# The gate with one column tile per pair and one transposition, the last group's results stored by halves, and another order of GpSimd's work, in a two-layer conditioned block

## The chip, the core and the metric

The kernel runs on one core of a Trainium2 chip, as one launch. The metric is the device time of one execution in microseconds (us). Everything is fp32. A profile of one execution is at hand for the kernel before. In it the engines are called PE (TensorE, the matmuls), PEld (PE's weight loads), DVE (VectorE), ACT (ScalarE), POOL (GpSimd) and SP (the engine that issues most DMAs).

## What is computed

The input x is 128 samples of 64 channels by 1024 positions. Two layers follow each other, each with a residual:

```
x = x + ffn0(cond0(x))      # cond0: per-sample 64x64 channel mix; ffn0: rank-128 linear, plus a bias
x = x + ffn1(cond1(x))      # cond1: grouped conv of 9 taps, plus a context per sample
def ffn1(y):                # per row of 1024
    logits = y @ gate_w.T + expert_bias          # 4 experts
    one_hot = first maximum of logits
    z = y @ lora_A.T                             # 4 experts x rank 8
    return y @ W_up.T + (z * one_hot) @ lora_B
```

The change concerns ffn1: the gate (logits and z, then the choice of the expert), and how the results of ffn1 are added to x and stored.

## The kernel before

**Tiles.** Two samples make a "pair" tile of 128 rows by 1024; there are 64 pairs. Two pairs make a group d, and the main loop (L778) runs over 32 groups. PE's order, like that of every engine, is the order in which the program is written (`manual_schedule`): nothing is moved by a scheduler, and a wait at the head of an engine's queue holds back all behind it.

**One pass of the loop.** For group d it runs: the second matmul of layer 0 for pair 2d+5 (`layer0_out`, L413); the gate of group d (`gate`, L590); on GpSimd the bias of layer 0 for pairs 2d+6 and 2d+7 (`add_fbias`, L640) and the convolution's differences for pairs 2d+4 and 2d+5 (`differences`, L452); products 8 to 25 of ffn1 for group d (`products`, L542), with the turning of the chosen z (`turn`, L618) ahead of product 23; then `tiles` (L648), which holds the convolution of pairs 2d+4 and 2d+5, the matmuls of the next group's gate (`gate_in`, L571), the low-rank part of group d (`lora`, L625) and the results (`results`, L631); then the sums of the next group (`ffn_sums`, L530), loads two groups on, layer 0 of pairs 2d+6 and 2d+7, and products 0 to 7 of group d+1 in two parts.

**ffn1 by products.** The 1024x1024 weight is not multiplied plainly: a fast scheme of 26 block products of 128x256 (the table `PRODUCTS`, L83) takes sums of blocks of y (made by GpSimd) and sums of blocks of W. Product (r, u, w, ...) goes into part r of eight; two parts share a PSUM bank, so bank 0 holds parts 0 and 1, bank 1 parts 2 and 3, and so on. Banks 0 and 1 are the low and high columns of the first pair, banks 2 and 3 those of the second. Products 0 to 3 of a group open banks 1, 2, 3 and 1 again, in that order. Some products are followed by a copy from one part to another on ACT (`"copy"`), or by an add to x on DVE (`"x"`). Product 19 is followed by an ACT copy of part 0 to part 2. The last products are: 20 to bank 2, 21 to bank 3, 22 and 23 to bank 0, 24 to bank 3 and 25 to bank 1.

**The gate.** `gate_in` (L571) takes `gl`, the 36 columns of gate and lora_A padded to 64, as stationary operand. It has 64 columns, so it fills half of PE's columns, and the other half can work beside it. Eight matmuls, one for each eighth c of the channels, are 256 wide: both pairs. Those with even c go to PSUM rows 0 to 63, those with odd c to rows 64 to 127. So the result is in two halves, which have still to be added. ACT copies 128x256 to SBUF (`gate_out`, L586). `gate` (L590) then runs, for each of the two pairs, a matmul with this copy as stationary operand and `fold` as moving operand, a 128x36 matrix with two ones in each column: it turns rows into columns and adds the halves. Eight small DVE instructions (L598 to L614) choose the expert and mask z.

```
rows = slice(c % 2 * GT, (c % 2 + 1) * GT)                            # L576
nc.tensor.matmul(pt[:, t * GL : (t + 1) * GL], zg[:, t], fold, ...)   # L595
```

**Results.** `lora` adds four matmuls, one for each bank; `results` adds the banks to x on DVE in the order 1, 3, 2, 0, and SP stores each pair whole, 512 KB. The banks of a group have only one buffer, so the next group's product 0 waits for the add of bank 1, product 1 for that of bank 2 and product 2 for that of bank 3.

**GpSimd's queue** holds, for a pass: two biases (each waits for the load of its x), two differences of two instructions (each waits for the convolution's input X, which has gone through DRAM), 17 sums, and the issue of four loads.

Of the kernel before, what the change touches and what calls it, by code (L numbers as in the profile page):

```python
# [35 lines left out]
F32 = mybir.dt.float32  # L36
AF = mybir.ActivationFunctionType
ALU = mybir.AluOpType
# [3 lines left out]
P = 128  # L42
# [4 lines left out]
NC = L // P  # L47
# [7 lines left out]
GL = E + ER  # L55
# [4 lines left out]
GT = 64  # L60
# [49 lines left out]
)  # L110
NW = 26

PK = tuple(np.cumsum([0, P, P, 1, 1, P, 8, 8, CH, CH, E]).tolist())

# [2 lines left out]
def block(ctx: ExitStack, tc: tile.TileContext, a: dict, out: bass.AP):  # L117
    nc = tc.nc
    const = ctx.enter_context(tc.tile_pool(name="const", bufs=1))
# [11 lines left out]
    sp = ctx.enter_context(tc.tile_pool(name="sp", bufs=2))  # L131
# [16 lines left out]
    ident = const.tile([P, P], F32, name="ident")  # L148
    make_identity(nc, ident)

    xs, xts, bds, aggbs, ctxs = {}, {}, {}, {}, {}
# [9 lines left out]
    for i in range(NBD):  # L161
        t = const.tile([P, GP, 2, CH], F32, name=f"bd{i}")
# [46 lines left out]
    for i in range(NX):  # L209
        t = cvp.tile([P, BG, P + 1], F32, tag=f"X{i}", name=f"X{i}")  # L210
# [13 lines left out]
        sel,  # L224
        ident[:, : 2 * FIRST].rearrange("p (t b) -> p t b", b=2).unsqueeze(2).to_broadcast([P, FIRST, CH, 2]),
    )
    fold = const.tile([P, GL], F32, name="fold")
    nc.vector.tensor_tensor(fold, ident[:, :GL], ident[:, GT : GT + GL], ALU.add)
    aggd = dram.tile([NB, CH, CH], F32, name="aggd")
    ctxd = dram.tile([NB, CH], F32, name="ctxd")  # L230
    aggbd = dram.tile([NB, CH], F32, name="aggbd")
# [12 lines left out]
    def load_context(g):  # L244
        load_rows(g, ctxs, ctxd, "cx")
# [138 lines left out]
    lo, hi = slice(0, N), slice(N, L)  # L384
    xbs, z0s, yts, opened = {}, {}, {}, {}
    diffs, pms, m2s, pcs, zgs, ys = {}, {}, {}, {}, {}, {}
# [65 lines left out]
    def differences(pr):  # L452

        xt = X[pr % NX]
        diffs[pr] = tmp.tile([P, BG, 2, H], F32, tag=f"tmp{pr % 2}", name=f"df{pr}")
        at_even, at_odd, after = (
            xt[:, :, s : s + P].rearrange("p g (m two) -> p g m two", two=2)[:, :, :, i]
            for s, i in ((0, 0), (0, 1), (1, 1))
        )
        nc.gpsimd.tensor_tensor(diffs[pr][:, :, 0], at_even, at_odd, ALU.subtract)  # L460
        nc.gpsimd.tensor_tensor(diffs[pr][:, :, 1], after, at_odd, ALU.subtract)
# [80 lines left out]
    def products(d, first, end):  # L542
        if not first:
            opened[d] = [psb.tile([P, N], F32, tag=f"pb{i}", name=f"pb{i}_{d}") for i in range(4)]
        for r, u, w, new, _, then in PRODUCTS[first:end]:
            p = part(d, r)
            if new == 2:
                nc.vector.memset(p, 0.0)
            for c in range(QC):
                nc.tensor.matmul(  # L550
                    p, ys[d][u][:, c], W[:, w, c], start=new == 1 and c == 0, stop=c == QC - 1, skip_group_check=True
                )
            for kind, to, op in then:
                if kind == "dcopy":
                    nc.vector.tensor_copy(part(d, to), p)
                elif kind == "copy" and op == "+":
                    nc.scalar.copy(part(d, to), p)
                elif kind == "copy":
                    nc.scalar.activation(part(d, to), p, AF.Copy, scale=-1.0)
                elif kind == "add":  # L560
                    copy = sums.tile([P, NQ], F32, tag="v", name=f"v{d}_{to}")
                    nc.scalar.copy(copy, p)  # L562
                    combine(nc.vector, part(d, to), part(d, to), op, copy)
                else:
                    x = xs[2 * d + to // 4][:, to % 4 * NQ : (to % 4 + 1) * NQ]
                    if op == "+":
                        nc.vector.tensor_tensor(x, p, x, ALU.add)  # L567
                    else:
                        nc.vector.scalar_tensor_tensor(x, p, -1.0, x, ALU.mult, ALU.add)  # L569

    def gate_in(d):  # L571

        yt = yts[d]
        pg = bank(f"pg{d}")
        for c in range(NC):
            rows = slice(c % 2 * GT, (c % 2 + 1) * GT)  # L576
            nc.tensor.matmul(  # L577
                pg[rows, : 2 * P].rearrange("m (t r) -> m t r", t=2),
                gl[:, c, :],
                yt[:, :, c],  # L580
                start=c < 2,
                stop=c >= NC - 2,
            )
        return pg

    def gate_out(d, pg):  # L586
        zgs[d] = sp.tile([P, 2, P], F32, tag="zg", name=f"zg{d}")
        nc.scalar.copy(zgs[d].rearrange("p t r -> p (t r)"), pg[:, : 2 * P])

    def gate(d):  # L590

        zg = zgs.pop(d)
        pt = bank(f"pgt{d}")
        for t in range(2):
            nc.tensor.matmul(pt[:, t * GL : (t + 1) * GL], zg[:, t], fold, start=True, stop=True)  # L595
        pv = pt[:, : 2 * GL].rearrange("p (t c) -> p t c", t=2)
        lg = sp.tile([P, 2, E], F32, tag="lg", name=f"lg{d}")
        nc.vector.tensor_tensor(lg, pv[:, :, :E], ebias.unsqueeze(1).to_broadcast([P, 2, E]), ALU.add)  # L598
        mx = sp.tile([P, 2], F32, tag="mx", name=f"mx{d}")
        nc.vector.tensor_reduce(mx, lg, AX.X, ALU.max)  # L600
        sc = sp.tile([P, 2, E], F32, tag="sc", name=f"sc{d}")
        nc.vector.tensor_tensor(sc, lg, mx.unsqueeze(2).to_broadcast([P, 2, E]), ALU.is_equal)
        nc.vector.tensor_tensor(sc, sc, rank.unsqueeze(1).to_broadcast([P, 2, E]), ALU.mult)
        ms = sp.tile([P, 2], F32, tag="ms", name=f"ms{d}")
        nc.vector.tensor_reduce(ms, sc, AX.X, ALU.max)
        oh = sp.tile([P, 2, E], F32, tag="oh", name=f"oh{d}")
        nc.vector.tensor_tensor(oh, sc, ms.unsqueeze(2).to_broadcast([P, 2, E]), ALU.is_equal)
        zm = sp.tile([P, 2, 2, E, R], F32, tag="zm", name=f"zm{d}")
        for h in range(2):
            nc.vector.tensor_tensor(  # L610
                zm[:, :, h],
                pv[:, :, E:].rearrange("p t (e r) -> p t e r", e=E),
                oh.unsqueeze(3).to_broadcast([P, 2, E, R]),
                ALU.mult,  # L614
            )
        return zm

    def turn(d, zm):  # L618
        p = bank(f"pzt{d}")
        nc.tensor.transpose(p[:, :P], zm.rearrange("p t h e r -> p (t h e r)"), ident)  # L620
        zt = sp.tile([P, P], F32, tag="zt", name=f"zt{d}")
        nc.scalar.copy(zt, p[:, :P])
        return zt

    def lora(d, zt):  # L625

        for j, p in enumerate(opened[d]):
            rows = slice(j * ER, (j + 1) * ER)
            nc.tensor.matmul(p, zt[rows, :], lb[rows, :], start=False, stop=True, skip_group_check=True)  # L629

    def results(d):  # L631
        p = opened.pop(d)
        xa, xb = xs.pop(2 * d), xs.pop(2 * d + 1)
        for x, cols, b in ((xa, hi, p[1]), (xb, hi, p[3]), (xb, lo, p[2]), (xa, lo, p[0])):
            nc.vector.tensor_tensor(x[:, cols], b, x[:, cols], ALU.add)  # L635
        del yts[d], ys[d]
        nc.sync.dma_start(out[2 * d], xa)
        nc.sync.dma_start(out[2 * d + 1], xb)

    def add_fbias(pr, eng):  # L640
        eng.tensor_tensor(xs[pr], xs[pr], fbias, ALU.add)  # L641
# [67 lines left out]
    gl = loaded("gl", [P, NC, GT], eng=nc.scalar)  # L709
# [66 lines left out]
    zm = gate(0)  # L776
    first_products(2)
    for d in range(NPAIR // 2):  # L778
        more = d + 1 < NPAIR // 2
        ahead = [pr for pr in (2 * d + 6, 2 * d + 7) if pr < NPAIR]  # L780
        if d and 2 * d + 5 < NPAIR:
            layer0_out(2 * d + 5)
        if 2 * d + 5 < NPAIR:
            load_context(d + 2)
        if ahead:
            load_cond(d + 3)
        if d:
            zm = gate(d)
        for pr in ahead:
            add_fbias(pr, nc.gpsimd)  # L790
        for pr in (2 * d + 4, 2 * d + 5):
            if pr < NPAIR:
                differences(pr)
        if d:
            products(d, 8, 23)
        else:
            first_products(2)
        zt = turn(d, zm)
        if d:
            products(d, 23, 26)  # L800
        else:
            first_products(2)
        tiles(d, zt, 2 * d + 4, 2 * d + 5)
        if more:
            ffn_sums(d + 1)
        for pr in (2 * d + 8, 2 * d + 9):
            if pr < NPAIR:
                load_x(pr)
        for pr in ahead:
            layer0_in(pr)  # L810
        if ahead:
            layer0_mix(ahead[0])
        if more:
            products(d + 1, 0, 4)
        if ahead:
            layer0_out(ahead[0])
            layer0_mix(ahead[1])
        if more:
            products(d + 1, 4, 8)
# [100 lines left out]
```

## Time and profile before

| | |
|---|---|
| median of 3 runs | 1308.2 us (1304.94 to 1309.74) |
| the profiled execution's own time | 1297.41 us |
| its span, first to last instruction | 1295.6 us |
| mean granted PE clock | 0.996 |
| PE busy | 1269.5 us (98%) |
| DVE, POOL, ACT busy | 726.5, 724.1, 240.5 us (56%, 56%, 19%) |
| one pass of the loop, between two gates | 38.85 us |

The profile lists the busy time of each engine, the chain of work that ended last (followed back from the end, each piece to what released it), groups of instructions by line, and a timeline. A line such as "12.00 0.37 PE pgt L595 x4" of the chain tells the start, the length, the engine, the tile written, the line and the number of instructions. PE's busy time alone does not tell that PE is the bound, since its instructions overlap; the chain does. In the profile every fp32 matmul counts as two records and two weight loads.

### The profile page before, as it was taken

The page shows a single profiled execution, that of the slowest core. Times are in us where ns is not written, and L with a number is a line of the kernel's source. Part 1 is how long each engine was busy: PE and PEld are TensorE (multiplying, and loading weights), DVE is VectorE, ACT ScalarE, POOL GpSimd, SP SyncE. Part 2 cuts the span into 40 slices and gives each one's busy share as a digit, 9 for nine tenths or more (in the row PEclk, how much of TensorE's full clock was granted, in tenths as well). Part 3 has the DMA queues.
Part 4 walks back from the last instruction along what each step waited for, and adds up shares of the span by engine and source line. Part 5 has one row for each costly group of instructions (what it writes and reads, how often), then busy time and mean ns, then how long its engine had stood idle before and what let it go on. Part 6 is the DMA issues. An engine that isn't in the chain of part 4 may idle for free.

```text
span 1295.6 us, 22883 instructions
## 1 busy us (share of the span) xinstructions
PE 1269.5 (98%) x8839; PEld 1050.4 (81%) x8839; DVE 726.5 (56%) x1485; ACT 240.5 (19%) x593; POOL 724.1 (56%) x861
## 2 busy tenths in 40 slices
PE   8789999999999999999999999999999999999997
PEld 6568888888888888888888888888888888888876
DVE  6685555556556466556455555455556455556443
ACT  2241111211111111111111111111111111111111
POOL 2437656546656556666556656556566455666431
PEclk9999999999999999999999999999999999999999
DMA  9974444564444664444664444564444654444301
GB/s 315 304 178 147 142 117 118 172 171 148 141 110 123 173 173 147 141 116 117 173 173 147 141 111 122 173 173 147 134 122 119 173 173 141 144 111 125 102 33 65
DMA packets 183867, 189.66 MB, mean 146 GB/s; under 512 B 17360, under 2 KB 156624, under 8 KB 183248
## 3 DMA queue, kind: packets, MB, share of 16 engines
q1 hardware_dynamic: 165904, 121.61, 34.7%
q0 software_dynamic: 16128, 58.73, 14.1%
q10 hardware_dynamic: 1728, 7.87, 1.7%
q8 instruction: 71, 1.16, 0.4%
q14 instruction: 36, 0.29, 0.1%
HBM read 118.90 MB, written 69.27 MB: 145 GB/s over the span
## 4 chain that ended last, share of the span: by engine, by line
PE 94%; DMA 2%; DVE 2%; ACT 1%; issue 0%; POOL 0%; SPq 0%; DVEq 0%; ACTq 0%; POOLq 0%
PE pb L550 55%; PE pxb L392 9%; PE pd L423 8%; PE pc L506 8%; PE pm L468 4%; PE pg L577 4%; PE pb L629 3%; DMA x<-in_x 1%; PE pz L402 1%; DMA x1d<-x 1%; PE pgt L595 1%; DVE yt L518 0%; DVE m L483 0%; DVE x L635 0%; DVE w L205 0%
## 5 line engine op out<-in xcount | busy, mean ns | idle before, releaser
L550 PE MATMUL pb<-w,s 128*128 128x256 f32 x2432 | 557.1, 380 | 1.9 <-DVE w L205 0.6
L550 PEld LDWEIGHTS pb<-w,s 128*128 128x128 f32 x2432 | 458.6, 190 | 69.8 <-issue 3.2
L641 POOL TENSOR_TENSOR x<-x,ffn_bias 128x1024 f32<-128x1024 f32 x62 | 146.1, 2357 | 179.9 <-DMA x<-in_x 179.9
L550 PE MATMUL pb<-w,yt 128*128 128x256 f32 x896 | 228.0, 383 | 2.6 <-DVE x L635 1.8
L483 DVE TENSOR_TENSOR m<-pm,cx 64x512 f32<-64x512 f32 x124 | 85.4, 689 | 201.7 <-PE pm L468 198.8
L550 PEld LDWEIGHTS pb<-w,yt 128*128 128x128 f32 x896 | 162.9, 190 | 23.4 <-DVE x L635 3.4
L460 POOL TENSOR_TENSOR df<-X 128x512 f32<-128x512 f32 x62 | 64.5, 1041 | 210.0 <-DMA X<-x1d 206.6
L567 DVE TENSOR_TENSOR x<-pb,x 128x256 f32<-128x256 f32 x320 | 127.5, 420 | 94.4 <-PE pb L550 89.5
L205 POOL TENSOR_TENSOR s<-yt,s 128x256 f32<-128x256 f32 x224 | 163.8, 731 | 17.8 <-PE pb L550 2.8
L392 PEld LDWEIGHTS pxb<-B,xt 128*128 128x128 f32 x1024 | 119.7, 195 | 25.0 <-DVE yt L518 22.0
L518 DVE TENSOR_TENSOR yt<-pc,m 128x512 f32<-128x512 f32 x124 | 122.3, 1107 | 21.7 <-ACT m L486 19.5
L392 PE MATMUL pxb<-B,xt 128*128 128x128 f32 x1024 | 125.5, 281 | 0.3 <-PE pb L550 0.3
L423 PE MATMUL pd<-AT,z 128*128 128x512 f32 x256 | 122.2, 599 | 2.9 <-DVE z L410 1.3
L506 PEld LDWEIGHTS pc<-ws,df 128*64 128x64 f32 x1984 | 110.4, 137 | 6.0 <-POOL s L205 1.1
L506 PE MATMUL pc<-ws,df 128*64 128x128 f32 x1984 | 114.0, 273 | 1.3 <-DVE m L483 1.3
L424 DVE TENSOR_TENSOR x<-pd,x 128x512 f32<-128x512 f32 x128 | 88.4, 692 | 44.9 <-PE pd L423 36.3
L562 ACT COPY v<-pb 128x256 f32<-128x256 f32 x96 | 35.8, 373 | 384.3 <-PE pb L550 366.8
L205 POOL TENSOR_TENSOR s<-s,yt 128x256 f32<-128x256 f32 x128 | 93.4, 729 | 17.0 <-PE pzt L620 9.6
L486 ACT COPY m<-m 64x512 f32<-64x512 f32 x124 | 76.5, 617 | 135.5 <-DVE m L483 125.8
L205 POOL TENSOR_TENSOR s<-s,s 128x256 f32<-128x256 f32 x128 | 92.6, 734 | 5.0
L569 DVE SCALAR_TENSOR_TENSOR x<-pb,x 128x256 f32<-128x256 f32 x128 | 54.0, 422 | 63.9 <-PE pb L550 61.1
L635 DVE TENSOR_TENSOR x<-pb,x 128x512 f32<-128x512 f32 x128 | 79.2, 680 | 15.5 <-PE pb L629 15.5
(107 smaller groups left out, 943.5 us busy)
## 6 DMA issues: line engine op xcount, KB each, us to landing
x1d<-x SPq DMA_DIRECT2D x128, 256.0 KB, 5.0
X<-x1d SPq DMA_DIRECT2D x128, 256.0 KB, 4.3
out<-x SPq DMA_DIRECT2D x64, 512.0 KB, 3.8
xt<-in_xt POOLq DMA_DIRECT2D x56, 512.0 KB, 5.7
x<-in_x POOLq DMA_DIRECT2D x56, 512.0 KB, 6.3
cx<-ctxd SPq DMA_DIRECT2D x32, 128.0 KB, 4.2
w<-in_wq ACTq DMA_DIRECT2D x4, 1024.0 KB, 7.0
ab<-aggbd SPq DMA_DIRECT2D x30, 128.0 KB, 3.4
```

Source lines behind the costliest of these rows:

```text
L205: eng.tensor_tensor(to, x, y, ALU.add if op == "+" else ALU.subtract)
L392: nc.tensor.matmul(pxb[:, :P], xt[:, c, :], bt[:, c, :], start=(c == 0), stop=(c == NC - 1))
L423: nc.tensor.matmul(pd, z0, at[:, cols], start=True, stop=True)
L424: nc.vector.tensor_tensor(x[:, cols], pd, x[:, cols], ALU.add)
L483: nc.vector.tensor_tensor(by_group(m2[half, b]), by_group(pm[half]), context(pr, b, half), ALU.add)
L486: nc.scalar.copy(m2[other, b], m2[half, b])
L506: nc.tensor.matmul(pc[o * H : (o + 1) * H, cols], diffs[pr][:, 2 * g + b, o], ws[:, g, o], start=True, stop=True,)
L518: nc.vector.tensor_tensor(yt.rearrange("m q (o g two) -> m two g q o", two=2, g=NGC)[:, b], by_group(pcs.pop((pr, b))), context(pr, b) if ...
L550: nc.tensor.matmul(p, ys[d][u][:, c], W[:, w, c], start=new == 1 and c == 0, stop=c == QC - 1, skip_group_check=True)
L567: nc.vector.tensor_tensor(x, p, x, ALU.add)
L635: nc.vector.tensor_tensor(x[:, cols], b, x[:, cols], ALU.add)
L641: eng.tensor_tensor(xs[pr], xs[pr], fbias, ALU.add)
```

## The change

It has four parts.

- `gate_in` gives each pair a column tile of its own: for each c there are two matmuls of 128 columns, the first pair to PSUM rows 0 to 63, the second to rows 64 to 127, each summed over all eight c. `gate_out` copies 128x128 instead of 128x256.
- `gate` turns this tile with one transposition (128x128, the identity as moving operand) in place of the two matmuls with `fold`, which is no longer made.
- `results` adds the banks in the order 1, 2, 3, 0. In the last group, `last_products` takes the place of the products from 17 on, of `tiles` and of `results`: the turning comes ahead of product 17, `lora` ahead of product 20, and each bank is added and stored (256 KB, half of the columns of a pair) as soon as its last product is through: bank 2 after product 20, bank 0 after 23, bank 3 after 24 and bank 1 after 25.
- On GpSimd the biases of pairs 2d+6 and 2d+7 come between the differences of pair 2d+4 and those of pair 2d+5, where they came ahead of both.

```
+LAST = ((21, 2), (24, 0), (25, 3), (26, 1))
-    fold = const.tile([P, GL], F32, name="fold")
-    nc.vector.tensor_tensor(fold, ident[:, :GL], ident[:, GT : GT + GL], ALU.add)
...
         for c in range(NC):
-            rows = slice(c % 2 * GT, (c % 2 + 1) * GT)
-            nc.tensor.matmul(
-                pg[rows, : 2 * P].rearrange("m (t r) -> m t r", t=2),
-                gl[:, c, :],
-                yt[:, :, c],
-                start=c < 2,
-                stop=c >= NC - 2,
-            )
+            for t in range(2):
+                nc.tensor.matmul(
+                    pg[t * GT : (t + 1) * GT, :P], gl[:, c, :], yt[:, t, c], start=c == 0, stop=c == NC - 1
+                )
...
-        zgs[d] = sp.tile([P, 2, P], F32, tag="zg", name=f"zg{d}")
-        nc.scalar.copy(zgs[d].rearrange("p t r -> p (t r)"), pg[:, : 2 * P])
+        zgs[d] = sp.tile([P, P], F32, tag="zg", name=f"zg{d}")
+        nc.scalar.copy(zgs[d], pg[:, :P])
...
-        for t in range(2):
-            nc.tensor.matmul(pt[:, t * GL : (t + 1) * GL], zg[:, t], fold, start=True, stop=True)
-        pv = pt[:, : 2 * GL].rearrange("p (t c) -> p t c", t=2)
+        nc.tensor.transpose(pt[:, :P], zgs.pop(d), ident)
+        pv = pt[:, :P].rearrange("p (t c) -> p t c", t=2)[:, :, :GL]
...
-        for x, cols, b in ((xa, hi, p[1]), (xb, hi, p[3]), (xb, lo, p[2]), (xa, lo, p[0])):
+        for x, cols, b in ((xa, hi, p[1]), (xb, lo, p[2]), (xb, hi, p[3]), (xa, lo, p[0])):
...
+    def last_products(d, zm):
+
+        zt = turn(d, zm)
+        products(d, 17, LAST[0][0] - 1)
+        lora(d, zt)
+        at_ = LAST[0][0] - 1
+        for end, b in LAST:
+            products(d, at_, end)
+            at_ = end
+            x, cols = xs[2 * d + b // 2], (lo, hi)[b % 2]
+            nc.vector.tensor_tensor(x[:, cols], opened[d][b], x[:, cols], ALU.add)
+            nc.sync.dma_start(out[2 * d + b // 2][:, cols], x[:, cols])
...
-        for pr in ahead:
-            add_fbias(pr, nc.gpsimd)
-        for pr in (2 * d + 4, 2 * d + 5):
+        for pr, plus in zip((2 * d + 4, 2 * d + 5), (ahead, ())):
             if pr < NPAIR:
                 differences(pr)
+            for other in plus:
+                add_fbias(other, nc.gpsimd)
+        if not more:
+            products(d, 8, 17)
+            last_products(d, zm)
+            break
```

More of the change, by code (lines that the diff above doesn't have):

```diff
@@ L575, in gate_in @@
         for c in range(NC):
-            rows = slice(c % 2 * GT, (c % 2 + 1) * GT)
-            nc.tensor.matmul(
-                pg[rows, : 2 * P].rearrange("m (t r) -> m t r", t=2),
-                gl[:, c, :],
-                yt[:, :, c],
-                start=c < 2,
-                stop=c >= NC - 2,
-            )
+            for t in range(2):
+                nc.tensor.matmul(
+                    pg[t * GT : (t + 1) * GT, :P], gl[:, c, :], yt[:, t, c], start=c == 0, stop=c == NC - 1
+                )
         return pg
     def gate_out(d, pg):
-        zgs[d] = sp.tile([P, 2, P], F32, tag="zg", name=f"zg{d}")
-        nc.scalar.copy(zgs[d].rearrange("p t r -> p (t r)"), pg[:, : 2 * P])
+        zgs[d] = sp.tile([P, P], F32, tag="zg", name=f"zg{d}")
+        nc.scalar.copy(zgs[d], pg[:, :P])
     def gate(d):
-        zg = zgs.pop(d)
         pt = bank(f"pgt{d}")
-        for t in range(2):
-            nc.tensor.matmul(pt[:, t * GL : (t + 1) * GL], zg[:, t], fold, start=True, stop=True)
-        pv = pt[:, : 2 * GL].rearrange("p (t c) -> p t c", t=2)
+        nc.tensor.transpose(pt[:, :P], zgs.pop(d), ident)
+        pv = pt[:, :P].rearrange("p (t c) -> p t c", t=2)[:, :, :GL]
         lg = sp.tile([P, 2, E], F32, tag="lg", name=f"lg{d}")
```

## The prediction, written before the change was run

> **What bounds the kernel now.** I read the page first: busy times, then the chain that ended last.
>
> ```profile
> PE 1269.5 (98%) x8839; PEld 1050.4 (81%) x8839; DVE 726.5 (56%) x1485; ACT 240.5 (19%) x593; POOL 724.1 (56%) x861
> ...
> PE 94%; DMA 2%; DVE 2%; ACT 1%; issue 0%; POOL 0%; SPq 0%; DVEq 0%; ACTq 0%; POOLq 0%
> ```
>
> The chain is 94% PE. Next I read the chain of one pass in order of time (start, length, piece).
>
> ```profile
> 588.71 0.37 PE pgt L595 x4
> 589.07 13.03 PE pb L550 x60
> 602.10 0.11 PE pzt L620
> 602.21 2.59 PE pb L550 x12
> 604.80 1.90 PE pm L468 x32
> 606.71 1.73 PE pg L577 x16
> 608.43 3.49 PE pc L506 x64
> ```
>
> Nothing but PE stands in it, and the next gate comes 38.85 us later (627.55), as does every one from 121 us on up to 1210 us. What a pass loses on PE, the kernel loses. Before 97 us and after 1229 us the chain also runs over DVE, ACT and DMA, so there I read single rows. Third, the timeline of the end (start, length, engine, line; in brackets the idle time ahead of it on its engine, and what ended it):
>
> ```profile
> 1263.15 1.13 PE L550 MATMUL pb<-w,yt 128*128 128x256 f32 x4 [0.78 <-DVE x L635]
> 1264.43 2.83 PE L550 MATMUL pb<-w,s 128*128 128x256 f32 x12 [0.16 <-DVE x L635]
> ...
> 1281.56 0.36 ACT L557 COPY pb<-pb 128x256 f32<-128x256 f32 x1 [3.02 <-PE pb L550]
> ...
> 1286.74 1.14 PE L629 MATMUL pb<-lb,zt 32*128 32x512 f32 x8
> 1287.92 2.48 DVE L635 TENSOR_TENSOR x<-pb,x 128x512 f32<-128x512 f32 x4 [6.80 <-PE pb L629]
> 1290.43 0.33 SPq L637 DMA_DIRECT2D out<-x  x1
> 1290.81 0.43 SPq L638 DMA_DIRECT2D out<-x  x1
> ```
>
> The span ends at 1295.6, so 7.7 us follow PE's last work. Fourth, GpSimd's timeline of a pass:
>
> ```profile
> 585.51 2.35 POOL L641 TENSOR_TENSOR x<-x,ffn_bias 128x1024 f32<-128x1024 f32 x1 [3.08 <-DMA x<-in_x]
> 588.85 2.35 POOL L641 TENSOR_TENSOR x<-x,ffn_bias 128x1024 f32<-128x1024 f32 x1 [0.98 <-DMA x<-in_x]
> 595.11 1.04 POOL L460 TENSOR_TENSOR df<-X 128x512 f32<-128x512 f32 x1 [3.91 <-DMA X<-x1d]
> 596.11 1.04 POOL L461 TENSOR_TENSOR df<-X 128x512 f32<-128x512 f32 x1
> 600.98 1.04 POOL L460 TENSOR_TENSOR df<-X 128x512 f32<-128x512 f32 x1 [3.83 <-DMA X<-x1d]
> ```
>
> **The gate's turning.** The two matmuls with `fold` take 0.37 us of the chain (0.366 between the starts of the first of them, 588.54, and of the next product, 588.91). They are four records of 36 columns with four weight loads of 128 columns. The new transposition has the form of L620: an fp32 tile of 128x128, one record, 0.11 us of the chain (0.107 between starts, 1283.95 to 1284.06). That saves 0.26 us. Group 0's gate (90.3 us) lies where products wait for DVE, so 31 gates count: 31 x 0.26 = **-8.0**. What is late next is product 8 and those behind it: product 13 (593.23) has to wait for a DVE read that ended at 592.55, so 0.68 us of slack shrinks to 0.42. DVE's eight gate instructions stay; the copy on ACT falls from 0.36 to 0.27 (L622's size), beside PE work.
>
> **The gate's matmuls.** Sixteen records 256 wide become 32 records 128 wide, and 16 weight loads of 64 columns become 32. The trace of before has no such sum over two tiles 128 wide, but it has the same shape without the long sum: the convolution L506 (64-column loads, 128 wide, alternating halves) takes 3.49 / 64 = 54.5 ns per record, L468 1.90 / 32 = 59.5 ns. Today's is 1.73 / 16 = 108 ns, or 54 per 128 columns. The ends are 32 x 54.5 = 1.74 and 32 x 59.5 = 1.90 us for 1.73, so +0.01 to +0.17 per pass; in L468 0.10 us of its 1.90 is a pause ahead of its first record, so L506 is nearer, and I take 55 ns, +0.03. Over 30 passes (in group 29's the chain runs over DVE beside it): **+0.9**, ends +0.3 and +5.
>
> The Trainium skill (TensorE: Matmul & The Clock Gate, Part 3, The mechanism) says that a weight load runs beside a matmul in flight only if it is for another row group; two column tiles share all rows, so by it each of the 16 added loads would stand bare, which is rival C. L506 speaks against it here: one load per record, each shown with 137 ns, and still 54.5 ns from record to record.
>
> **Order of results.** While layer 0 follows `lora`, the adds are hidden: the fourth ends near 615.7, the next product starts at 616.83. After groups 29 and 30 nothing hides them. After group 30, product 0 waits for bank 1 (0.78, unchanged); product 1 starts 1.28 us later, since its bank 2 is added third. Added second, it is free at about 1263.8, and product 1 can start 0.86 us (four records of 216 ns) after product 0: 1264.01 for 1264.43. After group 29 it is the same (1235.75 and 1237.04). Together **-0.85**; ends 0 and -0.9.
>
> **The last group.** PE does the same work in another order. New is a wait: `lora` writes bank 0 behind product 19, whose part 0 ACT still copies. That copy ended at 1281.92; product 20 started at 1281.36. PE stands for some 0.6 us, with the rest of `lora` and products 20 to 25 queued behind it, and DVE's four adds and SP's stores behind those; with one more 0.1 us pause after `lora` (as ahead of L468) +0.7. After PE's last record one add remains for four: 0.68 for 2.48, -1.8. The other three lie beside products, 0.86 us apart against 0.68. Then the stores. The second 512 KB was issued 0.4 us after the last add, and 1.05 MB left the core from about 1291.2 to 1293.7; landing took 3.0 us from issue (median of the two). A 256 KB half of rows has no row: a 138 KB load landed in 2.2 us, the fastest whole store in 2.6, a scattered 256 KB (x1d) in 5.0. I take 2.35, between the first two, since rows of 2 KB are nearer to whole rows than to scattered pieces: -1.0 for what lands sooner than 0.4 + 3.0, and -0.2 for two stores no longer sharing the engines. Ends -1.9 and +1.6. Together **-2.3**, ends -3.0 and +0.5. SP's queue holds nothing else there.
>
> **GpSimd's order.** Each bias waits for its x (landed by 588.85), each difference for its X. The first difference still starts at 595.11; the biases follow from 597.1 to 601.9; the second difference starts at 601.9 for 600.98. So it, the 17 sums and the first load issued behind them (615.99) come 0.9 us later. Cover: PE uses the second difference from about 609.8 (ready 603.9); the first sums are wanted at 617.7 (ready near 606); the load at 618.88 waits for a store anyway (2.33 us of idling). The biased x is wanted at 622 (layer 0) and ready at 601.9. Cost **0**; without this cover 0.9 x 29 = +26. One thing gets easier: the gate's DVE instruction L602 takes 166 ns at best, 438 median and 2325 at most, and ends with a bias (589.74 + 1.49 = 591.23; the bias 591.20). A bias no longer lies there, so product 13's slack grows again. In group 0 the first difference waits for X until about 88.8 and bias 6 moves to 90.9 to 93.2, just ahead of L602 (93.72): 0, at most +2.3 once. `fold` goes from DVE at 1.9 us (0.19), ahead of a wait for loads: 0.
>
> **Sum:** -8.0 + 0.9 - 0.85 - 2.3 = -10.3 us. Against the profiled execution 1297.41 becomes 1287.1. The median of the runs shown stands 10.8 us above that execution; I take the same difference from it: 1308.2 - 10.3 = **1298 us**.
>
> **Rivals.**
>
> A, the forecast: -10.3. Its own ends are -8.3 + 0.3 - 0.9 - 3.0 = -12 and -8.0 + 5 + 0 + 0.5 = -2.5, so 1296 to 1306, most of it below 1301. For it: every priced row stands in the chain. Chance 0.78, of which 0.07 lies within 0.5%.
>
> B, the turning's gain does not arrive: PE comes to product 13, or to a later one, 0.26 us sooner and waits there for DVE, or the transposition of a tile just copied costs as much as the pair. Then -10.3 + 8.0 = -2.3, 1306. For it: DVE follows PE within 0.7 us at product 13. Against: 60 records in 13.03 us today leave no wait, L620 sits between the same products, and DVE's gate gets freer. Chance 0.13.
>
> C, slower: the two column tiles do not run beside each other when each sums into the same 128 columns with a load for every record, because a load waits for the matmul ahead. Place: L577's successor. Price: with load and stream in turn a record takes 107 ns (twice 53.5), 32 x 107 = 3.42 for 1.73, +1.69 x 30 = +51 in place of +0.9: 1308.2 - 10.3 + 50 = 1348. It decides from the point where 30 x 32 records lose the other 11.2 us: 11.7 ns each, at 66 ns per record. Against: L506 at 54.5 and L468 at 59.5. For: neither sums over more than one matmul. Chance 0.09.
>
> **Numbers.** Likeliest 1298. The range 1291 to 1306 takes in A with its ends and the few us by which single runs differ, and B; C is out. About 0.5% (6.5 us) is what a measurement of this kernel can tell from no change: faster 0.71, same 0.20 (B and A's upper end), slower 0.09.
>
> **What would show it.** In the profile after: a pass of 38.62 us; the gate's turning 0.11 in the chain; its matmuls x32 in 1.74 to 1.80; product 1 of groups 30 and 31 about 0.87 after product 0; a pause of 0.6 us ahead of the last `lora`; one DVE add and under 6 us behind PE's last record; L602 near 0.17 and the second difference 0.9 us later, with no PE wait for POOL. I am wrong if the matmuls take over 2.1 us, if a wait for DVE appears among products 8 to 16, or if the pass stays at 38.85.

## The result, and the profile after

The changed kernel takes 1288.0 us (median of 4 runs, 1286.11 to 1288.22) where the kernel before, beside it, takes 1308.0 (4 runs, 1304.94 to 1309.74): ratio 0.9866, 95% interval 0.9843 to 0.9889, so -1.3%, with the interval wholly below 1. Two later comparisons gave 0.9875 (0.9847 to 0.9904) and 0.9884 (0.9860 to 0.9908); there the kernel before had medians of 1303.9 and 1304.3, over 11 and 17 runs. The forecast was -10.3 us and 1298, range 1291 to 1306. The sign was right, the gain was larger than forecast, and the time fell 3 us below the range.

The first lines of the page after, with PE's busy time down by 9.6 us and PE still 93% of the chain:

```profile
PE 1259.9 (98%) x9255; PEld 1059.1 (82%) x9255; DVE 705.0 (55%) x1484; ACT 237.0 (18%) x593; POOL 721.8 (56%) x861
...
PE 93%; DMA 3%; DVE 2%; issue 0%; ACT 0%; SPq 0%; DVEq 0%
```

The chain of one pass after (start, length, piece):

```profile
589.48 0.11 PE pgt L588
589.59 12.95 PE pb L549 x60
602.54 0.11 PE pzt L613
602.65 2.59 PE pb L549 x12
605.24 1.90 PE pm L467 x32
607.14 1.75 PE pg L576 x32
608.89 3.49 PE pc L505 x64
...
628.01 0.11 PE pgt L588
```

Read it piece by piece against the one of before. The turning is 0.11, as forecast. The gate's matmuls are 1.75 for 1.73, as forecast. The 60 records of products behind the turning take 12.95 for 13.03, which was not forecast. The pass is 38.53 us (38.62 forecast).

GpSimd's timeline in that pass, with the two biases between the differences and the second difference 0.65 us later behind the turning than before (602.40 - 589.48 for 600.98 - 588.71); nothing waits for it:

```profile
595.77 1.04 POOL L459 TENSOR_TENSOR df<-X 128x512 f32<-128x512 f32 x1 [13.35 <-DMA X<-x1d]
596.78 1.03 POOL L460 TENSOR_TENSOR df<-X 128x512 f32<-128x512 f32 x1
597.77 4.66 POOL L647 TENSOR_TENSOR x<-x,ffn_bias 128x1024 f32<-128x1024 f32 x2
602.40 1.03 POOL L459 TENSOR_TENSOR df<-X 128x512 f32<-128x512 f32 x1
```

And the timeline of the end after: products 0 and 1 of the last group, then the wait of `lora` for ACT, the last add and the four stores, issued from 1278.80 on. The span ends at 1286.4.

```profile
1257.64 1.13 PE L549 MATMUL pb<-w,yt 128*128 128x256 f32 x4 [0.78 <-DVE x L628]
1258.61 2.75 PE L549 MATMUL pb<-w,s 128*128 128x256 f32 x12
...
1275.43 0.36 ACT L556 COPY pb<-pb 128x256 f32<-128x256 f32 x1 [2.33 <-PE pb L549]
...
1275.85 1.14 PE L622 MATMUL pb<-lb,zt 32*128 32x512 f32 x8 [0.45 <-ACT pb L556]
...
1278.80 4.65 SPq L644 DMA_DIRECT2D out<-x  x4
...
1282.40 0.69 DVE L643 TENSOR_TENSOR x<-pb,x 128x512 f32<-128x512 f32 x1 [0.17 <-PE pb L549]
```

**Where the time went.** The starts of the gate's turning cut each profile into three. Gates 1 to 29 bound 28 even passes; what follows is the end; what comes before is the start, in which the stretch from gate 0 to gate 1 scatters most. The last column tells whether the granted TensorE clock fell to half, for 3.4 or 6.8 us, from a point between 95 and 101 us on.

| kernel (one profile each) | median, us | ratio to before (95%) | gate 0 to 1 | 28 passes | end | clock halved near 98 us |
|---|---|---|---|---|---|---|
| before | 1308.0 | 1 | 31.20 | 1088.82 | 85.27 | no |
| before, again | 1304.5 | 1.0007 (0.9991 to 1.0024) | 35.07 | 1088.79 | 85.29 | yes |
| GpSimd's order alone | 1302.3 | 0.9989 (0.9971 to 1.0007) | 33.01 | 1087.75 | 85.31 | no |
| gate alone | 1297.3 | 0.9938 (0.9914 to 0.9962) | 36.07 | 1085.40 | 84.46 | yes |
| end alone | 1299.7 | 0.9971 (0.9956 to 0.9986) | 37.11 | 1088.88 | 81.49 | yes |
| gate and order | 1290.8 | 0.9891 (0.9872 to 0.9910) | 35.10 | 1078.93 | 84.52 | yes |
| gate and end | 1291.4 | 0.9907 (0.9879 to 0.9934) | 36.75 | 1083.36 | 80.56 | yes |
| **changed** | 1288.0 | 0.9866 (0.9843 to 0.9889) | 32.83 | 1078.93 | 80.55 | yes |
| changed, again | 1287.6 | 0.9875 (0.9847 to 0.9904) | 33.21 | 1078.93 | 80.54 | yes |
| changed, third time | 1289.1 | 0.9884 (0.9860 to 0.9908) | 32.14 | 1078.93 | 80.57 | yes |

The passes give 1078.93 - 1088.82 = -9.9 us and the end 80.55 - 85.27 = -4.7: together **-14.6**. In the first pair of profiles the start took 5.4 us back (gate 1 at 126.92 for 121.51), so the spans differ by 9.2 only. Of these 5.4, 3.8 lie ahead of gate 0 (94.09 for 90.31) and 1.6 behind it, where a bias held the first gate (its L595 took 1.77 us, elsewhere 0.17). The profile of before had the earliest gate 1 of the profiles of the kernel before: 125.4 in the second one, and, by estimate, near 128 in the median run (1304.3, less 1.8 us outside the span, less passes and end of the profile). So that first profile was a lucky execution, and a forecast made on it and moved to the median has to say what the difference of 10.8 us consists of.

### The profile page after: what moved, and what is told of

Same layout as the page of the kernel before. It is cut to its first block, busy times and chain, and to the rows that moved or that the text cites. A ratio compares the mean times of both kernels' runs of the same rounds, so it can differ in the third digit from the quotient of the medians.

```text
span 1286.4 us, 23722 instructions
## 1 busy us (share of the span) xinstructions
PE 1259.9 (98%) x9255; PEld 1059.1 (82%) x9255; DVE 705.0 (55%) x1484; ACT 237.0 (18%) x593; POOL 721.8 (56%) x861
## 4 chain that ended last, share of the span: by engine, by line
PE 93%; DMA 3%; DVE 2%; issue 0%; ACT 0%; SPq 0%; DVEq 0%
PE pb L549 55%; PE pxb L391 9%; PE pd L422 8%; PE pc L505 8%; PE pm L467 5%; PE pg L576 4%; PE pb L622 3%; DMA X<-x1d 1%; PE pz L401 1%; DMA x<-in_x 1%; DVE yt L517 1%; DMA x1d<-x 1%; DMA xt<-in_xt 0%; PE pc L496 0%; DVE m L482 0%
```

## The experiments

The theories are those of the expectations. S: the spread of the kernel before lies in the start. P: a bias on GpSimd holds up VectorE instructions that read two operands from SBUF, and with the shorter gate TensorE then waits.

**The kernel before again** (no edit).

> The kernel before, once more, to see where its unprofiled runs (median 1308) differ from its first profiled one (1297.4). Theory S (the start): the start up to the first full pass varies with the loads from execution to execution, and the first profile of before was a lucky one; then the first gate of a full pass (121.7 us in that profile) comes 5 to 10 us later here, and passes stay at 38.85 us. Theory P (the port): in most executions a bias on GpSimd holds up the gate on VectorE so long that TensorE waits, and passes of up to 39.2 us are seen. Ratio 1.000 by both.

Measured: 1304.5 beside 1304.3, ratio 1.0007. Its passes sum to 1088.79 as in the first profile; its gate 1 comes 3.9 us later, and gate 0 at the same time (90.35 for 90.31). So the difference between these two executions lies in the start, as S says; the slower ones, up to 1309.9, have no profile. Some passes do take 38.9 to 39.1, but that is 1.0 us in all over an even 28 x 38.85, where P needed ten.

What P describes is seen in the start, though. In the first gate two instructions of VectorE take 2.27 and 0.77 us where 0.17 is usual, beside a bias and a difference on GpSimd. Product 22 waits 2.85 us for a sum of weights (w) that VectorE makes behind the gate; in the first profile, where the first gate was not held, it waited 0.16. These 2.7 us are most of the 3.9.

```profile
93.86 2.35 POOL L641 TENSOR_TENSOR x<-x,ffn_bias 128x1024 f32<-128x1024 f32 x1 [4.91 <-DMA x<-in_x]
93.96 2.27 DVE L603 TENSOR_TENSOR sc<-sc,rank 128x8 f32<-128x8 f32 x1
...
98.36 2.04 PE L550 MATMUL pb<-w,s 128*128 128x256 f32 x4 [2.85 <-DVE w L205]
```

**GpSimd's order alone.**

```
-        for pr in ahead:
-            add_fbias(pr, nc.gpsimd)
-        for pr in (2 * d + 4, 2 * d + 5):
+        for pr, plus in zip((2 * d + 4, 2 * d + 5), (ahead, ())):
             if pr < NPAIR:
                 differences(pr)
+            for other in plus:
+                add_fbias(other, nc.gpsimd)
```

> The kernel before with the change of GpSimd's order alone. By my forecast 0 to +2 us. Theory S: 0 to +2 us against before. Theory P: -8 to -12 us, since the biases no longer lie beside the gate; passes of 38.85 without exception.

Measured: 0.9989 (0.9971 to 1.0007), not told from nothing. In the profile all passes are even: 28 take 1087.75, -1.05. The order by itself is worth 1 us in the passes.

**The gate alone** (the hunks of `gate_in`, `gate_out` and `gate`, and `fold` left out).

> The kernel before with the new gate alone (a column tile per pair and one transposition). By my forecast -7 us; by the profile after, where a pass went from 38.85 to 38.53, -9. Theory S: -7 to -9 us. Theory P: the same or less, as product 13 comes 0.3 us sooner and VectorE is still held up; a wait for VectorE among products 8 to 16 would be seen.

Measured: 0.9938 (0.9914 to 0.9962), -7 to -8 us. Half of the passes take 38.53, the others 38.8 to 39.15. In all of these 14 it is product 13 that starts late, by 0.2 to 0.5 us, and its second record by 0.1 more. The timeline of one of those, at its turning: the bias (POOL) starts at 167.97, the gate's L599 (DVE), which should take 0.17, ends with it at 170.35, and TensorE's product 13, to whose bank L567 still has a read to make, starts at 171.12, 0.3 us late (20 records of 216 ns after 166.48 would be 170.80).

```profile
167.97 2.35 POOL L633 TENSOR_TENSOR x<-x,ffn_bias 128x1024 f32<-128x1024 f32 x1 [1.12 <-DMA x<-in_x]
...
168.17 2.18 DVE L599 TENSOR_TENSOR oh<-sc,ms 128x8 f32<-128x8 f32 x1
...
170.65 0.41 DVE L567 SCALAR_TENSOR_TENSOR x<-pb,x 128x256 f32<-128x256 f32 x1
...
171.12 2.86 PE L548 MATMUL pb<-w,s 128*128 128x256 f32 x12 [0.15 <-DVE x L567]
```

The product had 0.68 us of slack in the pass of before that the forecast read. With a turning 0.3 us shorter it has less, and a bias that comes late enough uses it up. This is rival B of the forecast, in the gate without the order.

**The end alone** (the hunk of `results`, `last_products` and its call).

> The kernel before with the order of the results and the last group's stores by halves alone. By my forecast -3.2 us; by the profile after -4.5. Theories S and P agree: -3 to -5 us.

Measured: 0.9971 (0.9956 to 0.9986). In the profile the end is 3.8 us shorter than before (81.49 for 85.27), passes as before.

**Gate and order, with the old end** (both hunks above).

> The kernel before with the new gate and GpSimd's new order, and the old end. Theory P: the two parts need each other; passes of 38.53 without exception, -9.9 us over 28 passes and -0.9 in the last three, -10.8 against before, where the gate alone gave -7 and the order alone -2 (not told from nothing). If they only add up: -7 to -9, with passes as uneven as with the gate alone.

Measured: 0.9891 (0.9872 to 0.9910). 28 even passes of 38.53. Passes and end give -10.6; the rest of the -13.9 between the medians lies in neither. In the passes, the gate alone gave -3.4, the order alone -1.05, both -9.9: they need each other, as P says.

**Gate and end, with the old order** (the changed kernel with the first hunk undone).

> The changed kernel with GpSimd's order as before (biases ahead of both differences). Theory P (a bias beside the gate holds up its VectorE instructions that read twice from SBUF, and with the shorter gate TensorE then waits): +5 to +7 us against the changed kernel, -8 to -10 against before, and passes of about 38.75 on average, as in the run with the gate alone. My forecast, in which the order costs and gains nothing: the same as the changed kernel.

Measured: 1291.4 against 1287.6 for the changed kernel beside it, +3.8; the passes take 4.4 us more (1083.36), a little less than expected. My forecast, that the order neither costs nor gains, is refuted: the -8.0 us of the turning held only with it.

**The gate's tables in PSUM, with new gate, old order and old end.**

```
-        lg = sp.tile([P, 2, E], F32, tag="lg", name=f"lg{d}")
+        lg = pt[:, P : P + 2 * E].rearrange("p (t e) -> p t e", t=2)
...
-        sc = sp.tile([P, 2, E], F32, tag="sc", name=f"sc{d}")
+        sc = pt[:, P + 2 * E : P + 4 * E].rearrange("p (t e) -> p t e", t=2)
```

> The kernel before with the new gate and GpSimd's old order, but the gate's two small tables (the logits lg and the marks sc) in PSUM, so that each of its VectorE instructions reads at most one operand from SBUF. Theory P (the second SBUF input is what a bias shuts out): the three instructions take 0.2 us in every pass, passes of 38.53, -10 to -11 us against before. Rival L (the biases beside the gate cost in another way, as late loads or late differences): as with the gate alone, -7 us, with waits for VectorE in the chain.

Measured: 0.9893 (0.9864 to 0.9922), and 28 even passes, 1078.93. The biases stand beside the gate as before, and hold up nothing. First GpSimd's timeline, then VectorE's, of the same pass:

```profile
202.53 2.36 POOL L633 TENSOR_TENSOR x<-x,ffn_bias 128x1024 f32<-128x1024 f32 x1 [2.28 <-DMA x<-in_x]
```

```profile
202.68 0.17 DVE L597 TENSOR_REDUCE ms<-pgt 128x2 f32<-128x8 f32 x1
202.88 0.17 DVE L599 TENSOR_TENSOR oh<-pgt,ms 128x8 f32<-128x8 f32 x1
```

The instruction's line over all passes tells the same. Count, then shortest, median and longest in ns: first with the gate alone, then with the tables in PSUM.

```profile
L594 DVE TENSOR_TENSOR sc<-lg,mx x32: 166/1010/2345, 95.2 to 1273.8; 128x8 f32<-128x8 f32 x32
```

```profile
L594 DVE TENSOR_TENSOR pgt<-pgt,mx x32: 174/174/175, 96.0 to 1263.3; 128x8 f32<-128x8 f32 x32
```

Nothing else was changed, and the gate's instruction with one SBUF operand is not held with the gate alone either (L590, which writes `lg` to SBUF: 158 ns at most). So it is the second SBUF operand that a bias shuts out, and rival L is refuted. The Trainium skill (SBUF — State Buffer, section SBUF: two separate sides) has this as a lock: a VectorE instruction with two SBUF inputs and a GpSimd instruction that reads SBUF shut each other out for the whole instruction. By that rule the holds end with the bias, at most 2.36 us after they begin; the longest here is 2.345. The trace agrees.

**A plain matmul for the transposition.**

```
-        nc.tensor.transpose(pt[:, :P], zgs.pop(d), ident)
+        nc.tensor.matmul(pt[:, :P], zgs.pop(d), ident, start=True, stop=True)
```

> The changed kernel with a plain matmul by the identity in place of the transposition. If the price of the turning is that of its records: two records of 128 columns with full weight loads, 0.22 us (as L402 in the chain) for 0.11, so passes of 38.64. If it is the width of 36 against 128 that made the old one slow: 0.11, passes of 38.53.

Measured in its profile (one run, 1291.2 us): passes of 38.64 to 38.65, and in the chain

```profile
590.39 0.22 PE pgt L588 x2
590.61 12.95 PE pb L549 x60
```

So each 128-wide record costs 0.11, a plain fp32 matmul is two, the transposition one; and the products behind it take 12.95 here too. The 0.08 us that they lose behind the old turning goes with its four 36-wide records; whether by their width or by their number was not separated.

**The old order in the first pass alone.**

```
+        if not d:
+            for other in ahead:
+                add_fbias(other, nc.gpsimd)
-        for pr, plus in zip((2 * d + 4, 2 * d + 5), (ahead, ())):
+        for pr, plus in zip((2 * d + 4, 2 * d + 5), (ahead if d else (), ())):
```

> The changed kernel with GpSimd's old order in the first pass alone. In the profile after, the first gate's instruction took 1.78 us beside a bias, and the chain ran through it. If that is a loss: -1.6 us against the changed kernel. Rival: the start is bound by loads, 0.

Measured: 1285.8 (1283.23 to 1292.45) beside 1287.6; ratios 0.9869 and 0.9875 with intervals of 0.003 to each side. Inconclusive.

**The changed kernel with the two tables in PSUM**, first beside other kernels, then beside the changed kernel.

> The changed kernel with the gate's two small tables in PSUM. Passes are even already, so they stay at 38.53; the first gate, which a bias held for 1.6 us in the profile after, is free. Theory P: -1.6 us against the changed kernel, as with the old order in the first pass (-1.8 there, not told from nothing). Rival: 0, since the start is bound by loads and by VectorE's sums of weights.

> The changed kernel with the two tables in PSUM, on the same chip as the changed kernel: -2 to -5 us against it, all of it ahead of the first full pass (its first gate of a full pass came at 121.3 us, that of the changed kernel at 126.9).

> The changed kernel once more, since runs of the kernel before scatter by 10 us. By the phases of the two profiles, without the start that scatters: passes -9.9, end -4.7, so -14.6 us (-1.1%). My forecast was -10.3. If the first result (-20 us) is the change's own, -20.

> The changed kernel a third time, beside the next: -14.6 us by passes and end alone, -16 to -20 by the two results so far. It tells whether 2 us or more come from the start.

Measured: the changed kernel 0.9875 and 0.9884 (table), between the -14.6 us of passes and end and the -20 of the first comparison. With the tables in PSUM 1283.2, ratio to before 0.9839 (0.9818 to 0.9860), then 1284.8, 0.9853 (0.9828 to 0.9877), beside 1289.1 for the changed kernel. All passes and the end are the changed kernel's (1078.93, 80.56); gate 0 to gate 1 takes 31.24 both times. It is the fastest of these kernels, 4.4 us ahead by the medians of one chip, though the two intervals there overlap. That the tables gave all of this is not shown: in the two profiles gate 1 comes 4.3 us earlier (122.69 for 127.00), but 3.4 of it lies ahead of gate 0 (91.45 for 94.86), where both kernels run the same instructions.

**The two tables in PSUM in the kernel before.**

> The kernel before, old gate, old order and old end, with the gate's two small tables in PSUM alone. Theory P says what the biases cost the kernel before: its passes become even, 38.85, so -1.0 us over 28 passes. If the bias also lengthens the start (the first gate held up, and TensorE's clock halved for a window of 3.4 us near 98 us after that wait), up to -5 us. Rival: the start scatters for another reason, -1 us and the half clock near 98 us is seen as often.

Measured: 0.9975 (0.9961 to 0.9989), -1.4 to -5.1 us. 28 even passes, 1087.74: -1.05 as with the order alone. The rest, some 2 us, lies outside the passes as the profiles of the kernel before have them; in executions without a profile they may lose more. The twelve runs end at 1302.9 where the kernel before, beside it, reaches 1309.7.

**What stays open: the start.** Gate 0 to gate 1 takes 31.20 to 31.24 us in the six profiles in which the first gate was not held and the granted clock stayed whole near 98 us. Two things lengthen it. One is the hold of the first gate. With the order alone the clock stayed whole, one instruction of the first gate took 1.99 us, and the stretch took 33.01; with the gate alone three of them lost 3.6 us, and product 22 waited 3.71 us. The changed kernel's first gate was held in two of three profiles (1.77 and 2.17 us). The other is the clock, halved for one or two windows of 3.4 us: without a hold, one window made it 32.14 (the changed kernel the third time) and 32.15 (the old order in the first pass alone). Here are two windows of 3 us (length; busy time and count of PE, PEld, DVE, ACT and POOL; then granted clock, DMA share and GB/s), first of the changed kernel the third time, then with the tables in PSUM beside it.

```profile
97.00:100.00 3.00, 2.15 (x6) 1.64 (x6) 2.79 (x12) 1.75 (x4) 2.38 (x2) 0.70 1.18 167
100.00:103.00 3.00, 3.00 (x12) 2.44 (x12) 1.89 (x4) 0.36 (x2) 1.92 (x2) 0.73 0.58 82
```

```profile
97.00:100.00 3.00, 2.91 (x13) 2.01 (x12) 1.53 (x3) 0.27 (x1) 2.18 (x3) 1.00 0.17 41
100.00:103.00 3.00, 3.00 (x55) 2.99 (x56) 1.78 (x3) 1.02 (x2) 2.77 (x5) 1.00 0.02 5
```

The halving was in 9 of 12 profiles without the tables in PSUM and in none of 4 with them. In five of the nine product 22 waited 2.4 to 3.7 us for the held gate, with the halving during this wait or up to 1.3 us behind it. In the other four only two waits of 0.9 us, for products 20 and 21, lie ahead of it. That the held gate causes it is not shown. In the changed kernel the third time none of the three gate instructions with two SBUF operands was held (168 ns at most), and the clock was halved all the same. With the order alone product 22 waited 1.97 us, and it was not; nor was it behind the same two waits of 0.9 us in three profiles with the tables in PSUM.

The Trainium skill (TensorE: Matmul & The Clock Gate, section Why this matters for your kernels) asks for no gaps of TensorE over some 3 us; here the clock was halved behind gaps of 0.9 us in four executions, while the length of the windows, 3.4 us, is as its Part 1 has it. So 0.6 to 5.4 us of the measured -15 to -20 lie outside the passes and the end of the profiles, and whether the change or the luck of the start gave them is not settled.

## Why the prediction was right and wrong

By passes and end the change is worth -14.6 us where -10.3 was forecast. Two steps failed. The turning's term, -8.0, was mis-sized by 2.5, since it left out what the old turning did to the product behind it. And the term of GpSimd's order, 0, was wrong in its mechanism: the old order's biases hold VectorE so long, in some passes, that product 13's slack is gone and TensorE waits; the new order ends that. The last group was another 0.7 short and the gate's matmuls 0.3. That makes 4.3 us (rounding aside) of the 10 by which 1288.0 lies under 1298. The rest is the 10.8 us that the forecast added for the median: the changed kernel's runs stand only 5.2 above the first profile less the 14.6 (1297.4 - 14.6 = 1282.8).

- **The gate's turning, -8.0:** the 0.26 us is as forecast; the term was too small by 0.08. The step took the saving as "0.366 between the starts of the first of them, 588.54, and of the next product", and stopped there. The next product was itself slowed. The profile of before shows it: four records of a product take 1.11 us behind the turning and 1.03 elsewhere, and 60 take 13.03 where 12 take 2.59 (five times that is 12.95).

```profile
588.91 1.11 PE L550 MATMUL pb<-w,yt 128*128 128x256 f32 x4
...
603.78 1.03 PE L550 MATMUL pb<-w,yt 128*128 128x256 f32 x4
```

  0.08 over 31 gates is -2.5.
- **GpSimd's order and product 13's slack, 0:** the forecast read 0.68 us from one pass, took every pass up to 1210 us for 38.85, and let "its slack grows again" stand as an aside of the order, at cost 0. Both readings fail on its own profile: 5 of the 28 passes take 38.99 to 39.09 (1.0 us lost), each late at product 13, and the longest L602 that it quotes, 2325 ns, is 0.84 us more than the 1.49 of the pass that it read. With the new gate and the old order 14 of 28 passes are late (1085.40 - 1078.93 = 6.5 us lost). The order is what the turning's gain rests on: credited with nothing, it was worth 4.4 us in the passes with the new end and 6.5 without, the 1.0 us lost before among them.
- **The gate's matmuls, +0.9:** 1.75 for 1.73 per pass, +0.6. Rival C is refuted: 54.7 ns per record with a load for each, also when each half sums into the same 128 columns. The rule on row groups that the forecast cites (the Trainium skill, TensorE: Matmul & The Clock Gate, Part 3, The mechanism) does not describe these records: each load is shown with 137 ns, for the same rows, and none stands bare. The same section of the Trainium skill also lets the PE pull ahead a load for the background weight buffer; whether that is what happens, no run here shows.
- **Order of results, -0.85:** the passes from gate 29 to 30 and from gate 30 to 31 lose 0.41 and 0.40 in the run with the end alone. Right. In the timeline after, product 1 follows product 0 by 0.97 us, without a wait.
- **The last group, -2.3:** from gate 31 to the end of the span it is -3.3, of which the turning has 0.3: -3.0. The wait ahead of `lora` (0.45 for 0.6, with a pause behind it) and the adds were near the forecast. The stores were mis-sized: 2.0 us from issue to landing (median of the four) where 2.35 was taken; 3.3 us from the last add to the end for 5.2, -1.9 where -1.2 was taken.
- **GpSimd's delay, cost 0:** no wait for it in the passes. The first gate was held once, within the forecast's "at most +2.3 once": an instruction of 1.77 us in the first profile, 2.17 in the second, none in the third. That the kernel before is held there too, in some executions, the forecast did not see.
- **The step from execution to median:** adding 10.8 us to both sides took the start of one lucky profile for a constant. The profile after stands 0.2 us above its median. From the wider samples of the kernel before (1304) the same sum gives 1294 and the same ends 1287 to 1302, in which 1288.0 lies; that would have been luck, since the effect, -14.6 by passes and end, was still forecast nearly a third too small.

## What to carry to other kernels

When an instruction is taken out of a stream, compare the stretch that follows it with the same stretch elsewhere in the pass: what it does to its successor goes with it. When a stream gets shorter, look at the slack of each wait behind it over all passes, not in one, and at what holds up the engine that it waits for; a neighbour off the path can be what the gain rests on. And before a forecast is moved from one profile to a median, cut the profile into phases and ask which of them repeats.

## What was not expected of the hardware

In these traces a GpSimd tensor-tensor instruction over SBUF holds up a VectorE instruction with two SBUF operands to its own end (0.17 us become up to 2.35), and moving one operand to PSUM frees it (0.175 us at most) for 8 ns more than the 0.166 that it takes undisturbed. Four fp32 records of 36 columns with 128-column loads cost 0.37 us and 0.08 more in the product behind them. And two waits of 0.9 us within 3 us, with no longer one near, were followed by a halved TensorE clock for 3.4 us in four of 16 profiles; the same two waits in three others, and one of 1.97 us in another, were not.
